# A graph-network kernel with a new order of its steps: both halves of the scores side by side, layer-one sums directly ahead of their product, other first and last steps

## The chip, the core and the metric

The kernel runs on one core of a Trainium2 chip. The core has four compute engines with a queue of their own each: TensorE (PE, matrix products into PSUM; its weight loads are listed as PEld), VectorE (DVE), ScalarE (ACT) and GpSimd (POOL). SyncE (SP) issues the DMA transfers. Engines meet through semaphores, and each works through its queue in order. The metric is the device time of the core in microseconds (us), lower is better; the shown time is the median of three runs.

## What is computed

64 graphs of 256 nodes with 512 features go through two layers, the second of which is two graph attentions in a row. In short:

```
# layer 0: 8 heads of 64
Q, K, V = x @ W_q, x @ W_k, x @ W_v
scores = einsum('bihd,bjhd->bhij', Q, K) / 8 + bias(x @ w_g) + log(adj + 1e-9)
x = einsum('bhij,bjhd->bihd', softmax(scores), V) + x
# layer 1, twice: 8 heads with W1, then 1 head with W2
h = layer_norm(x) @ W
e = leaky_relu(s_i + t_j, 0.2) + adj        # s, t: h times two vectors, per head
x = einsum('bhij,bhjk->bhik', softmax(e), h) + x
```

All is float32.

## The kernel before

Each graph (a "batch") is one Python generator, `graph(b)`; a call of `next` on it emits one *step*. The steps of a batch have names: load, turn (transposes X and the adjacency), V, V7, V4, Q, Q7, Q4, K, K7, K4, two scores, two mask, sums 0, product 0, gather 0, tokens 1, V1, V1 7, V1 4, rows 1, eight weights, sums 1, product 1, gather 1, tokens 2, V2, V2 7, V2 4, rows 2, weights 2, two product 2. The digit 0 stands for layer 0, 1 for the first attention of layer 1, 2 for the second.

What each step does, with the lines of the profile:

- V, Q, K, V1 and V2 are 256x512 by 512x512 products done in seven half-size products (Strassen and Winograd, `winograd`, matmuls on L326 or L333). The main step makes products 1, 5, 2, 6 and 3; product 6 adds into the bank ps_a that product 1 wrote, and product 3 into ps_b, so each must wait for ScalarE's copy of that bank (m and u: L525, L558 or L639). The step ending in 7 makes product 7, again into ps_a, after the copy u of product 6; the one ending in 4 makes product 4 into ps_a, after VectorE has read product 7 (L537, L567, L575 or L648). ScalarE reads product 4 (L535, L646 and others).
- A scores step (L592) makes four heads: 64-row matmuls, two at a time in the two halves of the array, into four PSUM banks. ScalarE takes exp of each bank (L599).
- A mask step multiplies the exps of four heads with the adjacency (L613, 128x1024, two of them) and adds the two halves up (L618).
- sums (L384) makes the sums of the weights over the source nodes with 32-column matmuls, four at a time; VectorE inverts them (L390), and the result goes to DRAM (L393) and comes back spread over partitions as R (L398). It also fetches the stored x (L252), to which ScalarE adds a bias (L409).
- product (L425) is weights times values, also 32-column matmuls. gather scales it with R (L434), adds x (L438), transposes (L258), takes statistics (eight L263, L265), and GpSimd makes the sums and differences S for the next Winograd product (L302 to L305). In layer 1, GpSimd also adds a row to the transposed Z (L702), after L265.
- tokens finishes the statistics: one matmul (L268), some ten small VectorE operations (L273 to L290), and a power on GpSimd (L292) that gives rstd.
- V1 4 ends with L659, which rows 1 needs: L458, L460, four stores (L463) and two loads (L473) of R, 512 KB each. A buffer for R is one of three, and is free again when sums 1 of the batch before has read it.
- weights: relu (L676), plus adjacency (L682), exp (L686), and at the end of four heads the sum of the two halves, written over R (L691).
- weights 2 is two operations on VectorE (L744); product 2 (L756) ends with a reciprocal (L761), a scaled copy (L764), an addition on GpSimd (L765) and four stores of the output (L771).

The batches overlap like a pipeline. A list `period` holds (age, step) pairs: in period n, step s with age a is emitted for batch n - a. It is repeated for all batches, but the first periods are replaced by a list `start`, and the last by `finish`, where the batch is counted from the end. TensorE works in exactly the order of these lists (`manual_schedule`); for the other engines the framework's planner orders the instructions from priorities and its own estimate of durations, so their orders change when the list does. All PSUM tiles come from one ring of eight banks.

```
period = [
    (1, "V4"), (2, "mask"), (5, "V2"), (5, "V2 7"), (2, "sums 0"),
    (2, "product 0"), (5, "V2 4"), (1, "Q"), (5, "rows 2"), (4, "sums 1"),
...
```

Of the kernel before, what the change touches and what calls it, by code (L numbers as in the profile page):

```python
# [20 lines left out]
def kernel(  # L21
# [94 lines left out]
    def weight(name, more=0):  # L116
        return const.tile([P, 2, 7, HD + more], F32, name=name)
# [34 lines left out]
    with ExitStack() as main:  # L152
# [324 lines left out]
        def graph(b):  # L477
# [295 lines left out]


        period = [
            (1, "V4"), (2, "mask"), (5, "V2"), (5, "V2 7"), (2, "sums 0"),
            (2, "product 0"), (5, "V2 4"), (1, "Q"), (5, "rows 2"), (4, "sums 1"),
            (3, "weights"), (2, "gather 0"), (3, "weights"), (3, "weights"),
            (5, "weights 2"), (3, "weights"), (0, "turn"), (1, "Q7"), (4, "product 1"),
            (1, "Q4"), (1, "K"), (1, "K7"), (5, "product 2"), (1, "K4"), (3, "weights"),  # L780
            (5, "product 2"), (2, "tokens 1"), (0, "V"), (1, "scores"), (3, "weights"),
            (3, "weights"), (2, "V1"), (4, "gather 1"), (-1, "load"), (2, "V1 7"),
            (0, "V7"), (4, "tokens 2"), (2, "V1 4"), (1, "scores"), (1, "mask"),
            (2, "rows 1"), (2, "weights"),
        ]

        start = [
            (0, "load"), (0, "turn"), (0, "V"), (0, "V7"), (0, "V4"), (1, "load"),
            (0, "Q"), (1, "turn"), (0, "Q7"), (0, "Q4"), (2, "load"), (0, "K"),
            (0, "K7"), (0, "K4"), (0, "scores"), (1, "V"), (1, "V7"), (1, "V4"),  # L790
            (2, "turn"), ("w1", "transpose"), (0, "scores"), (0, "mask"), (0, "mask"),
            (1, "Q"), (0, "sums 0"), (1, "Q7"), (0, "product 0"), (0, "gather 0"),
            (1, "Q4"), (1, "K"), ("w1", "columns"), (3, "load"), (1, "K7"), (1, "K4"),
            (3, "turn"), (0, "tokens 1"), ("w1", "totals"), (1, "scores"), (2, "V"),
            (2, "V7"), (0, "V1"), ("w2", "transpose"), (1, "scores"), ("w2", "columns"),
            (0, "V1 7"), (0, "V1 4"), (1, "mask"), (1, "mask"), (1, "sums 0"),
            (2, "V4"), (2, "Q"), (0, "rows 1"), (2, "Q7"), (2, "Q4"), (1, "product 0"),
            (2, "K"), (0, "weights"), (1, "gather 0"), (2, "K7"), (0, "weights"),
            (1, "tokens 1"), (2, "K4"), (2, "scores"), (3, "V"), (2, "scores"),
            (1, "V1"), (2, "mask"), ("w2", "totals"), (2, "mask"), (1, "V1 7"),  # L800
            (0, "weights"), (4, "load"), (2, "sums 0"), (0, "weights"), (0, "weights"),
            (1, "V1 4"), (0, "weights"), (0, "weights"), (3, "V7"), (1, "rows 1"),
            (2, "product 0"), (1, "weights"), (3, "V4"), (0, "weights"), (3, "Q"),
            (5, "load"), (3, "Q7"), (4, "turn"), (2, "gather 0"), (0, "sums 1"),
            (3, "Q4"), (3, "K"), (3, "K7"), (1, "weights"), (0, "product 1"), (3, "K4"),
            (2, "tokens 1"), (4, "V"), (2, "V1"), (1, "weights"), (0, "gather 1"),
            (1, "weights"), (1, "weights"), (2, "V1 7"), (1, "weights"), (3, "scores"),
            (1, "weights"), (2, "V1 4"), (1, "weights"), (4, "V7"), (0, "tokens 2"),
            (3, "scores"), (3, "mask"), (2, "rows 1"), (2, "weights"),
        ]  # L810
        FOLDS = [(w, step) for w in ("w1", "w2") for step in ("transpose", "columns", "totals")]
        order = [
# [3 lines left out]
        ]  # L816

        finish = [
            (-3, "mask"), (-6, "V2"), (-2, "V4"), (-6, "V2 7"), (-3, "sums 0"),
            (-3, "product 0"), (-6, "V2 4"), (-2, "Q"), (-5, "sums 1"), (-4, "weights"),  # L820
            (-4, "weights"), (-2, "Q7"), (-6, "rows 2"), (-5, "product 1"),
            (-4, "weights"), (-1, "turn"), (-3, "gather 0"), (-2, "Q4"), (-2, "K"),
            (-6, "weights 2"), (-2, "K7"), (-4, "weights"), (-6, "product 2"),
            (-2, "K4"), (-3, "tokens 1"), (-4, "weights"), (-6, "product 2"), (-1, "V"),
            (-2, "scores"), (-3, "V1"), (-3, "V1 7"), (-1, "V7"), (-5, "gather 1"),
            (-5, "tokens 2"), (-3, "V1 4"), (-4, "weights"), (-2, "scores"),
            (-3, "rows 1"), (-1, "V4"), (-2, "mask"), (-5, "V2"), (-4, "weights"),
            (-2, "mask"), (-5, "V2 7"), (-2, "sums 0"), (-4, "sums 1"),
            (-2, "product 0"), (-5, "V2 4"), (-3, "weights"), (-2, "gather 0"),
            (-1, "Q"), (-5, "rows 2"), (-4, "product 1"), (-1, "Q7"), (-1, "Q4"),  # L830
            (-1, "K"), (-3, "weights"), (-2, "tokens 1"), (-5, "weights 2"),
            (-5, "product 2"), (-1, "K7"), (-5, "product 2"), (-2, "V1"), (-1, "K4"),
            (-3, "weights"), (-3, "weights"), (-2, "V1 7"), (-3, "weights"),
            (-1, "scores"), (-3, "weights"), (-3, "weights"), (-2, "V1 4"),
            (-2, "rows 1"), (-4, "gather 1"), (-4, "tokens 2"), (-1, "scores"),
            (-1, "mask"), (-2, "weights"), (-4, "V2"), (-1, "mask"), (-3, "weights"),
            (-4, "V2 7"), (-1, "sums 0"), (-1, "product 0"), (-4, "V2 4"),
            (-4, "rows 2"), (-2, "weights"), (-2, "weights"), (-3, "sums 1"),
            (-1, "gather 0"), (-4, "weights 2"), (-3, "product 1"), (-2, "weights"),
            (-4, "product 2"), (-1, "tokens 1"), (-3, "gather 1"), (-4, "product 2"),  # L840
            (-1, "V1"), (-1, "V1 7"), (-2, "weights"), (-1, "V1 4"), (-1, "rows 1"),
            (-3, "tokens 2"), (-2, "weights"), (-2, "weights"), (-3, "V2"),
            (-1, "weights"), (-3, "V2 7"), (-3, "V2 4"), (-3, "rows 2"),
            (-1, "weights"), (-2, "weights"), (-2, "sums 1"), (-1, "weights"),
            (-3, "weights 2"), (-2, "product 1"), (-1, "weights"), (-1, "weights"),
            (-3, "product 2"), (-3, "product 2"), (-1, "weights"), (-2, "gather 1"),
            (-1, "weights"), (-2, "tokens 2"), (-1, "weights"), (-1, "sums 1"),
            (-1, "product 1"), (-2, "V2"), (-2, "V2 7"), (-2, "V2 4"), (-2, "rows 2"),
            (-2, "weights 2"), (-2, "product 2"), (-1, "gather 1"), (-1, "tokens 2"),
            (-2, "product 2"), (-1, "V2"), (-1, "V2 7"), (-1, "V2 4"), (-1, "rows 2"),  # L850
            (-1, "weights 2"), (-1, "product 2"), (-1, "product 2"),
        ]
        whole = start + order[len(start) - len(FOLDS) : len(order) - len(finish)]
        whole += [(B + g, name) for g, name in finish]
# [3 lines left out]
        with tc.manual_schedule(engines={mybir.EngineType.PE}):  # L858
# [3 lines left out]
            w1, w2 = weight("w1", H), weight("w2", 1)  # L862
# [52 lines left out]
    with ExitStack() as rest:  # L915
# [6 lines left out]
        def tl(name, *shape):  # L922
            return pool.tile(list(shape), F32, name=name, tag=name)
# [108 lines left out]
        with tc.For_i(0, again) as b:  # L1032
# [40 lines left out]
            V = tl("Vr", P, NT, D)  # L1073
# [50 lines left out]
```

## Time and profile before

| what | value |
|---|---|
| median of 3 runs | 3265.06 us (3260.84 to 3265.26) |
| profiled execution, its own time | 3264.86 us |
| its span | 3263.1 us |
| mean granted TensorE clock | 0.991 |
| DMA, mean over the span | 125 GB/s |

The costliest groups of the page read: line, engine, operation, tile written and tiles read, shape, count, then busy time and mean duration in ns, and at last the time in which the engine stood still just before, with what ended most of it. Four of them:

| line, engine | count | mean ns | still before it |
|---|---|---|---|
| L613 DVE | 256 | 1670 | 77.4 us, for ACT L599 |
| L676 ACT | 1024 | 501 | 85.0 us, mostly for PE L425 |
| L599 ACT | 512 | 684 | 96.6 us, for PE L592 |
| L691 DVE | 128 | 1261 | 8.2 us, for ACT L686 |

The timeline lists, per engine, start and duration in us, the line, the tiles and how many records were merged. TensorE's records overlap, so the time that an item takes from the next is the difference of two starts. A matmul in float32 shows as two records. From 200 us to 3100 us the pattern repeats about every 49 us, one period.

### The profile page before, as it was taken

The numbers are of one execution on the slowest core, as the hardware profiler recorded it, in microseconds if no ns is written. First come the engines' busy times: TensorE is split into PE (matmuls) and PEld (weight loads), VectorE is DVE, ScalarE is ACT, GpSimd is POOL, SyncE is SP. The second block draws the span as 40 slices with busy tenths as digits, with TensorE's granted clock in tenths as the row PEclk, the third lists the DMA queues.
The fourth block names the chain that finished last, engine by engine and source line by source line (L and its number), as shares of the span: only waits on it lengthen the run. The fifth ranks groups of instructions, "written<-read, shape, count | busy, mean of one in ns | idle before, by whom it ended". The sixth has DMA issues, their size and how long they took to land.

```text
span 3263.1 us, 77828 instructions
## 1 busy us (share of the span) xinstructions
PE 3172.2 (97%) x28232; PEld 2604.9 (80%) x28232; DVE 2700.9 (83%) x6093; ACT 2192.0 (67%) x5959; POOL 1077.0 (33%) x1315
## 2 busy tenths in 40 slices
PE   7999999999999999999999999999999999999985
PEld 5788888888888888888888888888888888888863
DVE  4888888888888888888888888888888888888884
ACT  2567667667667667667677677677677676676673
POOL 2233333332332342332332332332332332332332
PEclk9999999999999999999999999999999999999997
DMA  4334434444443444444443344444344344334332
GB/s 130 100 120 129 133 120 131 130 123 129 126 129 123 130 128 124 132 129 123 132 126 126 126 131 128 126 129 129 124 127 132 123 127 134 124 121 136 121 111 79
DMA packets 354662, 407.92 MB, mean 125 GB/s; under 512 B 117840, under 2 KB 262496, under 8 KB 354272
## 3 DMA queue, kind: packets, MB, share of 16 engines
q1 hardware_dynamic: 353120, 401.83, 39.7%
q8 instruction: 224, 3.67, 0.5%
q14 instruction: 166, 1.36, 0.1%
q10 hardware_dynamic: 1152, 1.06, 0.1%
HBM read 266.83 MB, written 135.87 MB: 123 GB/s over the span
## 4 chain that ended last, share of the span: by engine, by line
PE 86%; ACT 4%; DMA 3%; DVE 2%; issue 1%; SPq 0%; POOL 0%; DVEq 0%; ACTq 0%; POOLq 0%
PE ps_a L326 21%; PE ps_a L333 13%; PE ps_num L425 11%; PE ps_b L326 10%; PE ps_sc L592 7%; PE ps_av L756 7%; PE ps_b L333 6%; PE ps_c L326 5%; PE ps_su L384 4%; PE ps_c L333 3%; DMA R<-kept 2%; ACT ET L676 2%; ACT ET L686 1%; PE ps_st L268 1%; DMA zT<-kept 0%
## 5 line engine op out<-in xcount | busy, mean ns | idle before, releaser
L682 DVE TENSOR_TENSOR ET<-ET,AT 128x512 f32<-128x512 f32 x512 | 345.2, 685 | 234.7 <-ACT ET L676 234.5
L676 ACT ACTIVATE ET<-R,f 128x256 f32<-128x256 f32 x1024 | 460.5, 501 | 85.0 <-PE ps_num L425 70.1
L613 DVE TENSOR_TENSOR ET<-ET,AT 128x1024 f32<-128x1024 f32 x256 | 422.8, 1670 | 77.4 <-ACT ET L599 77.4
L686 ACT ACTIVATE ET<-ET,ends 128x256 f32<-128x256 f32 x1024 | 468.2, 503 | 11.7 <-DVE ET L682 4.9
L425 PE MATMUL ps_num<-ET,V 128*32 128x256 f32 x8192 | 467.5, 380 | 0.0
L302 POOL TENSOR_TENSOR S<-yT 128x256 f32<-128x256 f32 x64 | 47.4, 740 | 1112.0 <-DVE yT L438 994.6
L765 POOL TENSOR_TENSOR X<-X,weighted 128x256 f32<-128x256 f32 x256 | 211.7, 836 | 598.9 <-ACT weighted L764 598.8
L425 PEld LDWEIGHTS ps_num<-ET,V 128*32 128x32 f32 x8192 | 258.5, 110 | 162.1 <-issue 0.8
L599 ACT ACTIVATE ET<-ps_sc,V 128x512 f32<-128x512 f32 x512 | 309.0, 684 | 96.6 <-PE ps_sc L592 96.6
L756 PE MATMUL ps_av<-V,ET 128*128 128x258 f32 (+1 forms) x1024 | 252.7, 392 | 22.8 <-DVE ET L744 22.8
L326 PE MATMUL ps_a<-w,S 128*128 128x264 f32 (+1 forms) x1024 | 267.9, 384 | 3.9 <-ACT m L639 3.7
L326 PE MATMUL ps_b<-w,S 128*128 128x264 f32 (+1 forms) x1024 | 266.5, 383 | 0.0
L592 PE MATMUL ps_sc<-QT,KT 64*128 64x256 f32 x2048 | 258.3, 391 | 0.0
L592 PEld LDWEIGHTS ps_sc<-QT,KT 64*128 64x128 f32 x2048 | 188.5, 187 | 60.1 <-issue 41.7
L756 PEld LDWEIGHTS ps_av<-V,ET 128*128 128x128 f32 x1024 | 191.2, 197 | 47.5 <-issue 17.2
L263 DVE BATCH_NORM_STATS2 parts<-Z 128x6 f32<-128x128 f32 x1024 | 227.0, 275 | 0.0
L326 PEld LDWEIGHTS ps_a<-w,S 128*128 128x128 f32 x1024 | 188.9, 190 | 42.0 <-ACT m L639 5.4
L326 PEld LDWEIGHTS ps_b<-w,S 128*128 128x128 f32 x1024 | 193.9, 189 | 31.1
L646 ACT ACTIVATE V<-ps_a,rstd 128x257 f32<-128x257 f32 (+1 forms) x128 | 60.0, 469 | 205.0 <-PE ps_a L326 205.0
L409 ACT ACTIVATE yT<-yT,columns 128x256 f32<-128x256 f32 x256 | 115.0, 498 | 115.9 <-DMA yT<-kept 115.8
L434 DVE TENSOR_TENSOR ps_num<-ps_num,R 128x512 f32<-128x512 f32 x256 | 170.9, 692 | 5.5 <-DMA R<-kept 3.4
L691 DVE TENSOR_TENSOR R<-ET 128x1024 f32<-128x1024 f32 x128 | 161.4, 1261 | 8.2 <-ACT ET L686 8.1
(175 smaller groups left out, 7281.5 us busy)
## 6 DMA issues: line engine op xcount, KB each, us to landing
R<-kept SPq DMA_DIRECT2D x128, 512.0 KB
X<-in_x_dram SPq DMA_DIRECT2D x256, 128.0 KB
kept<-xT SPq DMA_DIRECT2D x64, 512.0 KB
yT<-kept SPq DMA_DIRECT2D x64, 512.0 KB
R<-kept SPq DMA_DIRECT2D x512, 64.0 KB
kept<-yT SPq DMA_DIRECT2D x64, 512.0 KB
kept<-Z SPq DMA_DIRECT2D x64, 512.0 KB
X<-kept SPq DMA_DIRECT2D x512, 64.0 KB
```

Source lines behind the costliest of these rows:

```text
L263: nc.vector.bn_stats(parts[:, block].rearrange("p h c -> p (h c)"), Z[:, block, :])
L326: nc.tensor.matmul(to, A[:, kk, :], B[:, kk, :], start=(first and kk == 0), stop=(kk == 1), skip_group_check=not first,)
L333: nc.tensor.matmul(to[:, m * P : (m + 1) * P], B[:, kk, m * P : (m + 1) * P], A[:, kk, :], start=(first and m == kk == 0), stop=(kk == 1), ...
L425: nc.tensor.matmul(num[32 * a : 32 * a + 32, m * N : (m + 1) * N], V[:, j, a // 2, a % 2 * P + q * DH + 32 * m :][:, :32], pair[a // 2][:, ...
L592: nc.tensor.matmul(banks[h % 2][:, o : o + N], KT[lo : lo + DH, (q + h) // 2, j * P : (j + 1) * P], QT[lo : lo + DH, (q + h) // 2, :], sta ...
L599: nc.scalar.activation(ET[:, j, i::2, :], banks[i].rearrange("p (h n) -> p h n", n=N), AF.Exp, bias=c[:, j, :],)
L613: nc.vector.tensor_tensor(ET[:, j, :, :], ET[:, j, :, :], AT[:, j, :].unsqueeze(1).to_broadcast([P, 4, N]), ALU.mult,)
L676: nc.scalar.activation(ET[:, j, h, :], R[q][:, h, :], AF.Relu, bias=f[:, j, at : at + 1])
L682: nc.vector.tensor_tensor(two, two, AT[:, j, :].unsqueeze(1).to_broadcast([P, 2, N]), ALU.add)
L686: nc.scalar.activation(ET[:, j, i, :], ET[:, j, i, :], AF.Exp, bias=targets[:, j, 4 * q + i : 4 * q + i + 1],)
L756: nc.tensor.matmul(av[:, :width], ET[:, j, t * P : (t + 1) * P], V2[:, j, n, :width], start=(j == 0), stop=(j == NT - 1),)
L765: nc.gpsimd.tensor_tensor(o[:, cols], o[:, cols], weighted, ALU.add)
```

## The change

Only the three lists differ; no operation is added or removed. In `period`:

- the two scores steps of a batch follow one another directly (they stood before and after V1 with its step 7), and stand ahead of V4;
- sums 1 stands directly ahead of product 1 on TensorE (the steps between them issue nothing there); before, Q7 was between them;
- Q7 follows Q, since sums 1 no longer comes there;
- V1 follows V (before, a scores step was between them), and V1 4 comes before tokens 2 (before, after it);
- both mask steps come behind both scores;
- weights, turn and load take other places.

```diff
         period = [
-            (1, "V4"), (2, "mask"), (5, "V2"), (5, "V2 7"), (2, "sums 0"),
-            (2, "product 0"), (5, "V2 4"), (1, "Q"), (5, "rows 2"), (4, "sums 1"),
-            (3, "weights"), (2, "gather 0"), (3, "weights"), (3, "weights"),
-            (5, "weights 2"), (3, "weights"), (0, "turn"), (1, "Q7"), (4, "product 1"),
-            (1, "Q4"), (1, "K"), (1, "K7"), (5, "product 2"), (1, "K4"), (3, "weights"),
-            (5, "product 2"), (2, "tokens 1"), (0, "V"), (1, "scores"), (3, "weights"),
-            (3, "weights"), (2, "V1"), (4, "gather 1"), (-1, "load"), (2, "V1 7"),
-            (0, "V7"), (4, "tokens 2"), (2, "V1 4"), (1, "scores"), (1, "mask"),
-            (2, "rows 1"), (2, "weights"),
+            (3, "V1 4"), (5, "tokens 2"), (2, "scores"), (2, "scores"), (1, "V4"),
+            (3, "rows 1"), (2, "mask"), (5, "V2"), (3, "weights"), (2, "mask"),
+            (5, "V2 7"), (2, "sums 0"), (2, "product 0"), (5, "V2 4"), (1, "Q"),
+            (5, "rows 2"), (1, "Q7"), (4, "sums 1"), (2, "gather 0"), (3, "weights"),
+            (3, "weights"), (3, "weights"), (5, "weights 2"), (4, "product 1"),
+            (0, "turn"), (1, "Q4"), (1, "K"), (1, "K7"), (3, "weights"),
+            (5, "product 2"), (1, "K4"), (5, "product 2"), (3, "weights"),
+            (2, "tokens 1"), (0, "V"), (2, "V1"), (3, "weights"), (4, "gather 1"),
+            (2, "V1 7"), (0, "V7"), (-1, "load"), (3, "weights"),
         ]
```

The lists `start` and `finish` are rewritten in the same sense. In `start`, the first scores of batch 1 come ahead of tokens 1 of batch 0, and rows 1 of batch 0 comes sooner:

```diff
-            (3, "turn"), (0, "tokens 1"), ("w1", "totals"), (1, "scores"), (2, "V"),
-            (2, "V7"), (0, "V1"), ("w2", "transpose"), (1, "scores"), ("w2", "columns"),
...
+            ("w1", "columns"), (0, "gather 0"), (2, "turn"), (1, "K4"), (1, "scores"),
+            (0, "tokens 1"), (3, "load"), (2, "V"), ("w1", "totals"), (4, "load"),
+            (0, "V1"), (2, "V7"), (0, "V1 7"), (0, "V1 4"), (2, "V4"),
+            ("w2", "transpose"), (1, "scores"), ("w2", "columns"), (0, "rows 1"),
...
```

In `finish`, V2 of the batch before the last stands ahead of sums 1 of the last, and product 1 of the last behind V2 4:

```diff
-            (-1, "weights"), (-2, "tokens 2"), (-1, "weights"), (-1, "sums 1"),
-            (-1, "product 1"), (-2, "V2"), (-2, "V2 7"), (-2, "V2 4"), (-2, "rows 2"),
-            (-2, "weights 2"), (-2, "product 2"), (-1, "gather 1"), (-1, "tokens 2"),
...
+            (-2, "tokens 2"), (-3, "product 2"), (-2, "V2"), (-1, "weights"),
+            (-1, "weights"), (-1, "weights"), (-1, "sums 1"), (-2, "V2 7"),
+            (-2, "V2 4"), (-2, "rows 2"), (-2, "weights 2"), (-1, "product 1"),
+            (-1, "gather 1"), (-2, "product 2"), (-1, "tokens 2"), (-2, "product 2"),
...
```

## The prediction

> **What bounds the kernel now.** I read the busy table first, then the chain of waits, then TensorE's timeline over a period, then the same stretch on VectorE and GpSimd.
>
> ```profile
> PE 3172.2 (97%) x28232; PEld 2604.9 (80%) x28232; DVE 2700.9 (83%) x6093; ACT 2192.0 (67%) x5959; POOL 1077.0 (33%) x1315
> PE 86%; ACT 4%; DMA 3%; DVE 2%; issue 1%; SPq 0%; POOL 0%; DVEq 0%; ACTq 0%; POOLq 0%
> ```
>
> TensorE (PE) is busy 97% and is 86% of the chain that ended last. Gaps can't be the prize, so I look for time that is lost while PE counts as busy. The timeline of PE (start, duration, line, tiles, records) shows it when starts are subtracted:
>
> ```profile
> 1505.83 1.03 PE L326 MATMUL ps_b<-wv,S 128*128 128x257 f32 x4
> 1506.79 2.00 PE L592 MATMUL ps_sc<-QT,KT 64*128 64x256 f32 x16
> 1508.72 1.16 PE L326 MATMUL ps_a<-w,yT 128*128 128x264 f32 x4
> 1509.71 1.05 PE L326 MATMUL ps_b<-w,S 128*128 128x264 f32 x4
> ...
> 1524.43 1.08 PE L384 MATMUL ps_su<-total,ones 128*32 128x128 f32 x32
> 1525.33 3.64 PE L425 MATMUL ps_num<-ET,V 128*32 128x256 f32 x64
> 1528.89 1.13 PE L326 MATMUL ps_a<-w,zT 128*128 128x257 f32 x4
> ...
> 1533.44 1.06 PE L333 MATMUL ps_b<-S,wq 128*128 128x128 f32 x8
> 1534.42 1.08 PE L384 MATMUL ps_su<-R,ones 128*32 128x128 f32 x32
> 1535.43 1.16 PE L333 MATMUL ps_a<-S,wq 128*128 128x128 f32 x8
> 1536.52 3.66 PE L425 MATMUL ps_num<-ET,V 128*32 128x256 f32 x64
> 1540.11 1.16 PE L333 MATMUL ps_a<-xT,wq 128*128 128x128 f32 x8
> 1541.11 1.06 PE L333 MATMUL ps_a<-xT,wk 128*128 128x128 f32 x8
> ...
> 1544.55 1.16 PE L333 MATMUL ps_a<-S,wk 128*128 128x128 f32 x8 [0.59 <-ACT m L525]
> ```
>
> A product of 128x257 takes 0.87 from start to start in a run of its kind (1504.10, 1504.96, 1505.83), one of 128x264 0.89, one of wq or wk 0.89. Ahead of the scores (64 rows) it takes 0.96, behind them 0.99. Going into the 64-row or 32-column layout and back (an "excursion") costs about 0.1 each way, and some inside.
>
> **The saving.** *Scores.* Cut into three stretches, a scores step is 0.32 for its first pair of records, 1.30 for six pairs (0.216 each), 0.31 for the last. Two apart: 0.09 in + 1.93 + 0.10 out, twice = 4.24. Side by side: 0.09 + (0.32 + 14 x 0.216 + 0.31 = 3.65) + 0.10 = 3.84. Saved: 0.40 a batch. *Layer-one sums and product.* Before, 1533.44 to 1541.11 holds product 3 of Q, sums, product 7, L425 and product 4: 7.67. After: 0.89 + 0.98 (product 7, going in) + 0.90 (sums straight into L425, as at 1524.43) + 3.58 + 1.00 = 7.35. Saved: 0.32. In the built order, the tiled stretches fall from 321 to 199: 60 pairs of scores merge and 62 of the others. 60 x 0.40 + 62 x 0.32 = 43.8, say **44 us**. The Trainium skill (TensorEngine Tiling (Array Packing), Performance Considerations) speaks against it: tiling speeds up TensorE, not the emptying of PSUM, which can then be the bottleneck. By that rule the two steps would last as long as ScalarE's eight exps: four at L599 take 2.42, eight some 4.75, against 3.65, so 1.1 x 60 = 66 us would be lost and the change be 22 slower. The row: at 0.58 an exp from 1.17 after the first matmul (1506.79, 1507.96) a bank is free at 1.85, and only the eighth bank (V's ps_a is held, seven are free) needs one, for the last quarter at 2.7. V4 behind them needs none, V2's three come after 4.6. So PE runs ahead and I take no stall; ScalarE's lag turns up below.
>
> **What the new order exposes.** Positions in us from V's first product, from the slots above: before, scores 4.4, V1 6.3, V1 4 12.9, scores 13.9, V2 16.7, layer-one sums 32.0, K 38.7. After: V1 4.4, V7 9.7, V1 4 10.6, statistics (L268) 11.5, both scores 11.8, V4 15.5, V2 16.4, layer-zero sums 21.7, Q 27.2, layer-one sums 32.6, K 38.1. A missed start costs the lateness and 0.1 for restarting (K's products after the 0.59 wait take 0.99).
>
> *(1) V1 directly behind V.* The scores no longer stand between, 1.93 of cover. Product 6 of V1, at 7.08, adds into ps_a and needs its copy (L639, 0.48). ScalarE's new order has the last two L686 ahead of that copy, and they need the last L682, which VectorE now has behind all eight L263 of zT. VectorE's small operations there meet GpSimd:
>
> ```profile
> 2049.71 3.15 DVE L613 TENSOR_TENSOR ET<-ET,AT 128x1024 f32<-128x1024 f32 x1 [0.16 <-ACT ET L599]
> 2049.41 2.36 POOL L702 TENSOR_TENSOR Z<-Z,bw 128x1024 f32<-128x1024 f32 x1 [0.60 <-DVE parts L263]
> 2059.62 1.23 DVE L613 TENSOR_TENSOR ET<-ET,AT 128x1024 f32<-128x1024 f32 x1 [1.01 <-ACT ET L599]
> ```
>
> The same L613 takes 3.15 beside L702 and 1.23 without. The Trainium skill (SBUF — State Buffer, section "SBUF: two separate sides") calls that port pair an exclusive lock, kept for a whole instruction. The rows' sum, unblocked: L258 1.16, two L768 0.1, eight L263 1.6, the statistics 0.6 and L537 0.34 from -0.45 put L682 (0.6) at 3.4 to 4.0, the copy done at 6.0 behind V1's own first product: no wait. By the lock, L768, L284, L285 and L288 each wait out what is left of one of GpSimd's 0.72 operations (L303 to L765, 0.0 to 4.2), some 1.8 together: L682 ends near 5.85, two L686 at 6.85, the copy at 7.3. I take **0.3** (0.2 late, 0.1 restart); ends 0 and 0.9 (every one a full turn late).
>
> *(2) L691 and the three L648.* L691 comes behind L265, which releases L702, so it takes some 3 instead of 1.26; L648 for V1 4 ends at 10.7 against 10.6. With (1) PE is itself 0.3 late: 0; ends 0 and 0.3.
>
> *(3) Layer-zero sums.* All mask work now stands behind the pair: from 2.46 after the scores' start four L613 and two L618 at 1.14 a turn, without L702, bound by exps 2 and 8, end at 9.5; the sums come at 9.9. If GpSimd's S for zT holds VectorE's small chain as now (2.6 against 1.4), 9.9: **0.05**; ends 0 and 0.3. Gone is the 2.36-long block of L613 by L702, worth nothing, since PE did not wait for it.
>
> *(4) Q7 directly behind Q.* Before, the sums (1.01) lay between and covered u (L558, two of 0.31). Product 6 ends 0.16 after its slot, u 0.62 and its signal later: 0.85 of 0.89, too late for loading weights ahead. **0.15**; ends 0 and 0.25.
>
> *(5) Layer-one R.* The layer-one sums release the buffer that SP's second L473 waits for; queued behind it are L473 of layer two, L393, yT's store and four L398, whose R VectorE's L434 takes 8.6 later. Sums end at 33.5 instead of 33.05, K is 0.6 earlier: 1.1 less room. But between R's landing and K's first copy ScalarE now has four L676 and two L686 instead of five and four, 1.2 less. K's present stall (a mean period of 49.17, from the layer-zero sums at 197.07 and 3097.92 over 59 periods, against 48.80 from 2016.15 to 2064.95) stays: 0; ends -0.2 and 0.2. The other moved issues (load, and the out-stores, 1 and 7 around xT's store instead of 2 and 6) stand in front of transfers for which PE never waits in the waits view: 0.
>
> *(6) First and last steps.* In the first 200 us PE waits about 31, in the last 110 about 40. Scores of batch 1 now cover part of the 3.9 wait at 84.17, while V1 of batch 0 comes nearer to its folded weights: 0. At the end V2 of batch -2 runs ahead of the last product instead of after (3209 instead of 3215), but the last sums come as much later: -4; ends -12 and +8.
>
> Sum: 3264.86 (profiled run; span 3263.1) - 44 + 60 x 0.50 - 4 = **3247 us**, -0.55%. The profiled run lies 0.2 under the shown median 3265.06, so no shift.
>
> **The rivals.** *A, cover holds:* VectorE and ScalarE keep ahead, only Q7's 0.15 stays: 3264.9 - 44 + 9 - 4 = 3226. For it: VectorE has slack (83%) and L691 leaves the stretch ahead of V. Against: the lock's row. *B, slower:* the chain L682, L686, copy, product 6. If L682 starts behind L702 or every small operation waits out a GpSimd turn, (1) is 0.9, the sums 0.3 and Q7 0.15, with 0.05 more at V1 4: 1.4 x 60 = 84, so 3265 - 44 + 84 - 4 = 3301. It decides from 0.8 a batch on. For it: five of 0.72 in a row; against: the operations now waiting mostly slip into the next gap. *C, nothing shown:* the waits move along with PE to R's landing, 0.75 a batch in all: 3264.9 - 44 + 45 - 4 = 3262. For it: the 0.59 wait in K; against: room computed in (5).
>
> **How the numbers follow.** Forecast 0.43 (3232 to 3258), A 0.17, B 0.27, C 0.13. Measurements of this kernel tell 0.2% (6.5 us) from no change. Faster: 0.43 + 0.17 = 0.60; same 0.13; slower 0.27. The range leaves out the lower part of A and B's upper half: 3214 to 3292.
>
> **What would show it.** Right: two scores steps together last 3.65, L384 goes into L425 after 0.90 both times, and product 6 of V1 starts 0.2 to 0.4 late behind ACT m L639. A: that start is on time, the period 48.1 to 48.2. B: PE waits for ACT m L639 or DVE total L618 over 0.6 a period. Wrong altogether, if sums and L425 side by side keep 1.01 and 3.59.

## The result, and the profile after

The changed kernel takes **3236.28 us** (median of 4 runs, 3234.22 to 3239.5), the kernel before in the same comparison 3265.16 (4 runs, 3260.84 to 3266.13): a ratio of 0.9915, 95% interval [0.9898, 0.9932]. The forecast was 3247: the right side, 11 us too slow. The profiled execution's span went from 3263.1 to 3232.4 at the same granted clock, 0.991.

The busy table and the chain of the page after, which answer to the two lines shown first in the prediction, and two of its groups (busy, mean ns, idle time before and its releaser):

```profile
PE 3135.6 (97%) x28232; PEld 2621.6 (81%) x28232; DVE 2717.1 (84%) x6093; ACT 2188.5 (68%) x5959; POOL 1068.4 (33%) x1315
...
PE 1%; DVE 1%; DMA 0%; ACT 0%; SPq 0%; issue 0%; POOL 0%; DVEq 0%
...
L686 ACT ACTIVATE ET<-ET,ends 128x256 f32<-128x256 f32 x1024 | 482.1, 503 | 104.7 <-DVE ET L682 103.6
...
L613 DVE TENSOR_TENSOR ET<-ET,AT 128x1024 f32<-128x1024 f32 x256 | 306.6, 1231 | 39.4 <-ACT ET L599 39.4
```

TensorE is busy 36.6 us less (3172.2 before) with the same 28232 matmuls, and still 97% of the span: what went was time inside "busy". The chain is of no use this time: it could be followed back over some 2% of the span only. Two groups changed: ScalarE's L686 now waits 103.6 us for VectorE's L682 (4.9 before), and L613 fell from 1670 to 1231 ns a piece.

TensorE's timeline of the kernel after, in one period (start, duration, line, tiles, records):

```profile
2016.95 1.14 PE L333 MATMUL ps_a<-S,wq 128*128 128x128 f32 x8
2018.03 1.08 PE L384 MATMUL ps_su<-R,ones 128*32 128x128 f32 x32
2018.93 3.64 PE L425 MATMUL ps_num<-ET,V 128*32 128x256 f32 x64
2022.49 1.16 PE L333 MATMUL ps_a<-xT,wq 128*128 128x128 f32 x8
2023.49 1.06 PE L333 MATMUL ps_a<-xT,wk 128*128 128x128 f32 x8
2024.38 1.06 PE L333 MATMUL ps_b<-S,wk 128*128 128x128 f32 x8
2025.28 1.06 PE L333 MATMUL ps_c<-xT,wk 128*128 128x128 f32 x8
2027.18 1.16 PE L333 MATMUL ps_a<-S,wk 128*128 128x128 f32 x8 [0.85 <-ACT m L525]
...
2040.82 1.05 PE L326 MATMUL ps_c<-w,yT 128*128 128x264 f32 x4
2041.71 1.05 PE L326 MATMUL ps_a<-w,S 128*128 128x264 f32 x4
...
2046.14 0.32 PE L268 MATMUL ps_st<-parts,same 128*128 128x48 f32 x2
2046.39 3.72 PE L592 MATMUL ps_sc<-QT,KT 64*128 64x256 f32 x32
```

Subtract starts. Q7 starts on time, 0.89 after the product ahead of it; from Q7 to the sums is 1.08, the sums go into L425 after 0.90, and L425 takes 3.56 to the next product: the three figures of the merge. Product 6 of V1 (2041.71) comes 0.89 after product 2: it does not wait. Product 6 of K (2027.18) comes 1.90 after product 2, where 0.89 is its clean slot.

The same subtraction, as the mean of the 51 periods between 400 and 2900 us, with what the prediction's slots and latenesses come to:

| slot (start to next start), us | before | after | forecast |
|---|---|---|---|
| two scores steps, without entry and exit | 2 x 1.93 | 3.654 | 3.65 |
| Q7 to layer-one sums | - | 1.074 | 1.13 |
| layer-one sums, layer-zero sums, each to the next item | 1.01 (Q7), 0.90 | 0.897, 0.897 | 0.90 |
| product 2 to 6 of V1 (copy L639) | 0.89 | 0.890 | 1.19 |
| V1 4 and L268, up to the scores | 1.21 | 1.14 | - |
| K, products 2 to L756 (four slots) | 4.07 | 4.27 | 4.07 |

The mean period, from the third product of one V to that of the next over 55 periods, fell from 49.165 to 48.702, by 0.463; over some 58 periods that is 26.9 of the 30.7 by which the span fell. The rest comes from the two ends: the third product of the sixth V lies at 232.8 instead of 225.5 (7.3 lost), and from that of the last V to the end it takes 174.7 instead of 185.9 (11.2 gained).

Where did the new stall in K come from? ScalarE's timeline of the kernel after, around the same product 6 of K (in brackets: idle time before, and its releaser):

```profile
2022.14 0.91 ACT L686 ACTIVATE ET<-ET,ends 128x256 f32<-128x256 f32 x2 [0.33 <-DVE ET L682]
2023.86 1.71 ACT L676 ACTIVATE ET<-R,f 128x256 f32<-128x256 f32 x4 [0.81 <-DMA R<-kept]
2025.47 0.90 ACT L686 ACTIVATE ET<-ET,ends 128x256 f32<-128x256 f32 x2
2026.27 0.60 ACT L558 ACTIVATE QT<-ps_a,columns 128x128 f32<-128x128 f32 x2
2026.77 0.36 ACT L525 COPY m<-ps_a 128x256 f32<-128x256 f32 x1
2027.02 0.38 ACT L525 COPY m<-ps_b 128x256 f32<-128x256 f32 x1
2027.29 0.52 ACT L686 ACTIVATE ET<-ET,ends 128x256 f32<-128x256 f32 x1
2027.70 0.72 ACT L517 ACTIVATE AT<-AT,eps 128x512 f32<-128x512 f32 x1
2028.31 0.51 ACT L686 ACTIVATE ET<-ET,ends 128x256 f32<-128x256 f32 x1
2028.71 0.37 ACT L525 COPY u<-ps_a 128x256 f32<-128x256 f32 x1
```

K's first product ended near 2024.5, but its copy m ran at 2026.77, behind four L676 of the second half (which waited for R's landing at 2023.86), two L686 of the first half and two copies of QT. Before, in the period that the prediction shows (K's first product started at 1541.11), ScalarE's row was this:

```profile
1540.03 2.11 ACT L676 ACTIVATE ET<-R,f 128x256 f32<-128x256 f32 x5 [0.84 <-DMA R<-kept]
1542.04 1.69 ACT L686 ACTIVATE ET<-ET,ends 128x256 f32<-128x256 f32 x4
1543.63 0.60 ACT L558 ACTIVATE QT<-ps_a,columns 128x128 f32<-128x128 f32 x2
1544.13 0.36 ACT L525 COPY m<-ps_a 128x256 f32<-128x256 f32 x1
```

From the first L676 behind R to copy m the row is shorter now, 2.91 instead of 4.10, as (5) forecast. But that L676 starts 0.37 after K's first product instead of 1.08 ahead of it. R's landing can be dated in every period by the semaphore that this L676 waits for: on average it came 1.67 ahead of K's first product before, and comes 0.28 ahead now, 1.39 later. In the kernel after, the slot with the wait for m follows the landing closely (correlation 0.97 over 52 periods). In 38 of these periods the row starts within 0.05 of the landing; in the other 14 R is there, and the row starts directly behind the two L686 that stand ahead of it.

The waits of ScalarE, in total, times and longest, for the kernel after; before they were 4.9 (6 times) and 13.6 (20 times):

```profile
ACT ET L686 <- DVE ET L682: 103.6, 120, 2.1
ACT ET L676 <- DMA R<-kept: 18.9, 26, 3.4
```

The first total misleads when it is read as K's. By place in the period, 79 of the 103.6 us (59 waits) lie 15 to 17 us behind K's first product, ahead of V1's copies, where TensorE does not wait (slot 0.890). Ahead of K there are 17.5 us, 52 waits of 0.34, all before the row that starts with R's L676.

So there were four theories of K's stall to part. **T1**: the landing of R. **T2**: VectorE's L682 come late and hold L686, which hold the copies. **T3**: only the place of m in ScalarE's queue. **T4**, formed on the way: ScalarE's whole row of work from R's landing to u.

### The profile page after: what moved, and what is told of

Its sections match the earlier page's. It is cut to its first block, busy times and chain, and to the rows that moved or that the text cites. A ratio compares the mean times of both kernels' runs of the same rounds, so it can differ in the third digit from the quotient of the medians.

```text
span 3232.4 us, 77827 instructions
## 1 busy us (share of the span) xinstructions
PE 3135.6 (97%) x28232; PEld 2621.6 (81%) x28232; DVE 2717.1 (84%) x6093; ACT 2188.5 (68%) x5959; POOL 1068.4 (33%) x1315
## 5 line engine op out<-in xcount | busy, mean ns | idle before, releaser
L682 DVE TENSOR_TENSOR ET<-ET,AT 128x512 f32<-128x512 f32 x512 | 363.4, 711 | 239.3 <-ACT ET L676 238.7
L686 ACT ACTIVATE ET<-ET,ends 128x256 f32<-128x256 f32 x1024 | 482.1, 503 | 104.7 <-DVE ET L682 103.6
L676 ACT ACTIVATE ET<-R,f 128x256 f32<-128x256 f32 x1024 | 461.3, 501 | 74.9 <-PE ps_num L425 55.7
L425 PE MATMUL ps_num<-ET,V 128*32 128x256 f32 x8192 | 466.7, 379 | 0.0
L765 POOL TENSOR_TENSOR X<-X,weighted 128x256 f32<-128x256 f32 x256 | 210.9, 834 | 545.0 <-ACT weighted L764 536.9
L425 PEld LDWEIGHTS ps_num<-ET,V 128*32 128x32 f32 x8192 | 263.9, 110 | 155.2 <-issue 1.1
L613 DVE TENSOR_TENSOR ET<-ET,AT 128x1024 f32<-128x1024 f32 x256 | 306.6, 1231 | 39.4 <-ACT ET L599 39.4
L599 ACT ACTIVATE ET<-ps_sc,V 128x512 f32<-128x512 f32 x512 | 302.3, 697 | 7.8 <-PE ps_sc L592 7.8
L756 PE MATMUL ps_av<-V,ET 128*128 128x258 f32 (+1 forms) x1024 | 250.7, 389 | 24.3 <-DVE ET L744 24.3
L592 PE MATMUL ps_sc<-QT,KT 64*128 64x256 f32 x2048 | 239.4, 383 | 0.0
L263 DVE BATCH_NORM_STATS2 parts<-Z 128x6 f32<-128x128 f32 x1024 | 238.3, 275 | 0.1
L756 PEld LDWEIGHTS ps_av<-V,ET 128*128 128x128 f32 x1024 | 189.8, 196 | 48.9 <-issue 13.0
L326 PEld LDWEIGHTS ps_a<-w,S 128*128 128x128 f32 x1024 | 185.9, 189 | 46.7 <-ACT m L639 6.9
L702 POOL TENSOR_TENSOR Z<-Z,bw 128x1024 f32<-128x1024 f32 x64 | 175.7, 2745 | 4.1 <-DVE parts L263 3.0
```

Of the source, the lines that this page charges most:

```text
L263: nc.vector.bn_stats(parts[:, block].rearrange("p h c -> p (h c)"), Z[:, block, :])
L326: nc.tensor.matmul(to, A[:, kk, :], B[:, kk, :], start=(first and kk == 0), stop=(kk == 1), skip_group_check=not first,)
L425: nc.tensor.matmul(num[32 * a : 32 * a + 32, m * N : (m + 1) * N], V[:, j, a // 2, a % 2 * P + q * DH + 32 * m :][:, :32], pair[a // 2][:, ...
L592: nc.tensor.matmul(banks[h % 2][:, o : o + N], KT[lo : lo + DH, (q + h) // 2, j * P : (j + 1) * P], QT[lo : lo + DH, (q + h) // 2, :], sta ...
L599: nc.scalar.activation(ET[:, j, i::2, :], banks[i].rearrange("p (h n) -> p h n", n=N), AF.Exp, bias=c[:, j, :],)
L613: nc.vector.tensor_tensor(ET[:, j, :, :], ET[:, j, :, :], AT[:, j, :].unsqueeze(1).to_broadcast([P, 4, N]), ALU.mult,)
```

## The experiments

All times are medians of several runs; each ratio is to the kernel before on the same chip, with its 95% interval. The kernel before read 3262 to 3268 in these comparisons, so compare ratios. Lines of a kernel with added code are shifted by a few.

### Is the saving the layout?

**One scores pair taken apart again**, with V4 between; everything else as after.

```diff
-            (2, "scores"), (2, "scores"), (1, "V4"),
+            (2, "scores"), (1, "V4"), (2, "scores"),
```

> The changed kernel with one step moved: V4 stands between the two scores steps instead of behind them, so that TensorE leaves the 64-row layout and returns once more in each period. Theory (going into and out of a tiled layout costs 0.40 us for the scores): 60 periods x 0.40 = 24 us more than the changed kernel, some 3260 us, and two scores steps of 1.93 in place of one of 3.65. Rival (the change gains by other waits, and the layout is not what is paid): within 5 us of the changed kernel's 3236.

Measured: 3262.71, ratio 1.0001 [0.9991, 1.0010]; mean period 49.130, 0.43 more than after, and K's slots and ScalarE's waits nearly as after. By its own slots the pair is worth 0.40 a period (the rest is mostly K's slots, 4.33 here): 23 to 25 of the 29 us.

**Layer-one sums apart from their product again**, with Q7 between, as before.

```diff
-            (5, "rows 2"), (1, "Q7"), (4, "sums 1"), (2, "gather 0"), (3, "weights"),
+            (5, "rows 2"), (4, "sums 1"), (1, "Q7"), (2, "gather 0"), (3, "weights"),
```

> The changed kernel with the layer-one sums back between Q and Q7; Q7 then stands between sums and product again. Theory of the layout: +0.32 a period, less 0.09 for the late start of Q7 that goes, so +0.23 x 62 = 14 us if the stall in K stays; the sums come 1.0 us sooner, so if K's stall comes from the R that waits for them, K's first copy is up to 1.0 sooner and the stall (0.43 a period in the changed kernel) goes: then -12 us or so against the changed kernel's stall, a sum of about 3238. If the stall in K comes from VectorE alone, 3250.

Measured: 3251.07, ratio 0.9962 [0.9948, 0.9976]; mean period 48.934, 0.23 more than after. That is the merge of 0.32 less the 0.09 by which Q7 takes longer directly behind Q. K's four slots together stayed (4.29), though R now landed 1.65 ahead of K's first product (0.28 in the kernel after): the first wait shrank (its slot 1.33 to 1.01), as T1 has it, and the wait of product 7 for u took its place (0.96 to 1.34), ScalarE's row behind R being longer in this order. So an earlier R alone does not shorten K.

### What holds K?

**The second R fetched as two transfers of two heads each**, so that the first heads land sooner.

```diff
-                nc.sync.dma_start(out=R, in_=kept[q : q + n, :].partition_broadcast(P))
+                for i in range(0, n, 2 if q else n):
+                    m = min(2, n) if q else n
+                    nc.sync.dma_start(
+                        out=R[:, i : i + m], in_=kept[q + i : q + i + m, :].partition_broadcast(P)
+                    )
```

> The changed kernel, with the second R of a batch loaded in two transfers of two heads each instead of one of four, so that its first half lands about 2 us sooner after the layer-one sums. Theory T1 (the stall in K of the changed kernel is the landing of R): ScalarE's waits for R (18.9 us) nearly go, and the stall in K falls from 0.43 to 0.1 a period: -15 to -20 us, about 3219. Theory T2 (it is VectorE's late L682, behind L258 and under GpSimd's lock): the stall stays within 0.1, the time within 5 us of 3236; one more issue on SP costs nothing that shows.

Measured: 3262.9, ratio 0.9998 [0.9988, 1.0008]. ScalarE waits longer for R, not shorter: 44.3 us in 59 waits (18.9 in 26). The planner, told that R's first heads come sooner, put their L676 sooner, and they waited. K's four slots went from 4.27 to 4.74; 0.47 x 60 = 28 accounts for the whole loss against the kernel after. The run missed both expectations and settles nothing between T1 and T2, but shows that ScalarE's built order decides.

**gather 0 listed behind three weights steps**, to let VectorE's L682 run ahead of it. TensorE's order is that of after.

```diff
-            (4, "sums 1"), (2, "gather 0"), (3, "weights"),
-            (3, "weights"), (3, "weights"), (5, "weights 2"),
+            (4, "sums 1"), (3, "weights"), (3, "weights"),
+            (3, "weights"), (2, "gather 0"), (5, "weights 2"),
```

> The changed kernel with gather 0 listed two weights steps later. TensorE's order is the same; the planner gives VectorE's L682 of these weights a place ahead of L258 and the eight L263, and ScalarE its four L686 before the second R. T2 (ScalarE waits for VectorE's L682: 103.6 us in the changed kernel, 4.9 in the one before): these waits in K fall below half, K's stall from 0.43 to about 0.2 a period, some 3222. T1 (R's landing): waits for R stay or grow, the stall in K stays above 0.35, 3236.

Measured: 3271.16, ratio 1.0029 [1.0018, 1.0040]. TensorE's wait in K in this kernel:

```profile
PE ps_a L333 <- ACT u L525: 60.8, 59, 1.1
```

The wait for m is gone (slot 0.90), R is waited for 4.9 us only, and now product 7 waits for u in every period (slot 2.11): in the built order four L676, an L686 and L517 stand between K's first copy and u. Four slots of K: 4.91. R lands as late as in the kernel after (0.24 ahead of K's first product, 0.28 there), but ScalarE now comes to the L676 that need it later than that, so that they rarely wait. The stall is larger without any wait for R: T1 cannot be the whole of it. This is where T3 came from.

**Sums directly behind Q, Q7 behind product 1.**

```diff
-            (5, "rows 2"), (1, "Q7"), (4, "sums 1"), (2, "gather 0"), (3, "weights"),
+            (5, "rows 2"), (4, "sums 1"), (2, "gather 0"), (3, "weights"),
...
-            (0, "turn"), (1, "Q4"), (1, "K"), (1, "K7"), (3, "weights"),
+            (0, "turn"), (1, "Q7"), (1, "K"), (1, "Q4"), (1, "K7"), (3, "weights"),
```

> The order after, with sums 1 directly behind Q (as in the Q7 trial), so R's buffer is free sooner, Q7 between turn and K (its copy u covered by product 1), and Q4 between K and K7. PE's layout changes are as in the order after. T3 (what makes K late is the place of K's copies in ScalarE's queue, behind second-half L676 that wait for R): in the built order K's copy m now stands behind eight L676 of the second half instead of four, so K waits more, and with it product 7 behind u: period 48.9 to 49.2, time 3248 to 3266. Rival T1 (R's landing alone): sums a product earlier give R 0.9 more room, the wait in K falls by 0.3 a period: 3218.

Measured: 3469.06, ratio 1.0637 [1.0619, 1.0655]. One premise was wrong: a batch emits its steps in its own order whatever their names in the list, so what ran was Q7, Q4, K, K7. TensorE's timeline of this kernel:

```profile
2065.62 1.16 PE L333 MATMUL ps_a<-S,wq 128*128 128x128 f32 x8
2069.07 1.16 PE L333 MATMUL ps_a<-xT,wq 128*128 128x128 f32 x8 [2.29 <-DVE QT L567]
...
2086.13 1.05 PE L326 MATMUL ps_c<-w,yT 128*128 128x264 f32 x4
2088.21 1.16 PE L326 MATMUL ps_a<-w,S 128*128 128x264 f32 x4 [1.03 <-ACT m L639]
```

Two covers are gone. Product 4 of Q stands directly behind product 7 and waits for VectorE to read it (3.47 instead of 0.89); and product 6 of V1 waits for copy m L639 in every period (2.08 instead of 0.89). It is the product whose wait the prediction priced at 0.3 and made rival B of, but the way there is another: the copy waits for rstd (L292; 213.6 us in 63 waits), which waits for the statistics, and among these L285, an operation on two elements a partition, now runs beside GpSimd's L702:

```profile
2083.63 2.28 DVE L285 SCALAR_TENSOR_TENSOR var<-means,var 128x2 f32<-128x2 f32 x1
```

It took about 2.28 in 58 of its 128 executions and 0.12 to 0.15 in most others. The two lost covers make 3.8 of the 4.1 by which the mean period grew, to 52.79. K's own slots fell to 3.91, but this says little about T3.

**The second half's L676 kept behind K's copies.** An edge of issue order on ScalarE alone; no data is waited for less. In one run they come behind the second m, in the other behind u.

```diff
...
+                    behind = [m for m in copies if len(m) > 1] if at >= 4 else []
+                    with tc.issue_after(behind[-1][1]) if behind else nullcontext():
-                    for j in range(NT):
+                        for j in range(NT):
...
```

> The order after, and one edge of issue order on ScalarE: no L676 of the second half is issued ahead of K's second copy m (the one product 3 needs). It takes no wait for data away and does not touch R, its buffer or VectorE's work. T3 (place in the queue): the wait for R no longer stands ahead of m, K's stall (0.45 a period over the clean 0.89) goes but for what the copies of QT and the last two L686 of the first half leave: period 48.3 to 48.4, time 3213 to 3219. Rival T1 (R's landing): the same lateness is paid behind m instead, by copy u or by the L682 and L686 that V1's copies stand behind: 3230 to 3240. Rival T2 (L682 late on VectorE holds L686, and L686 the copies): two L686 still stand ahead of m: 3225 to 3236.

> As the run before, but no L676 of the second half is issued ahead of K's copy u either (the one product 7 needs); they come some 2.6 later. T3: K's products wait for nothing but L686 of the first half: period 48.25 to 48.35, 3210 to 3216, unless the second half's later L682 and L686 now hold the copies of V and V1 (they stand between them in the built order): then up to 0.4 a period is paid there, 3216 to 3236. T1: no gain, 3230 to 3240.

Measured: 3472.57, ratio 1.0648 [1.0630, 1.0665], and 3453.21, ratio 1.0579 [1.0561, 1.0596]. No theory had this. In K, T3 was right for the first wait: its slot fell from 1.33 to 0.94 and 0.95. In the first run the wait went over to u (product 3's slot 0.96 to 1.43, four slots 4.39); behind u as well, the four slots make 3.84. But the planner then laid VectorE's work out anew. TensorE's timeline at V1 of the second run, and VectorE's and GpSimd's beside it:

```profile
2074.38 1.03 PE L326 MATMUL ps_a<-wv,S 128*128 128x257 f32 x4
2077.71 1.16 PE L326 MATMUL ps_a<-w,yT 128*128 128x264 f32 x4 [2.30 <-DVE V L656]
```
```profile
2073.36 1.44 DVE L263 BATCH_NORM_STATS2 parts<-Z 128x6 f32<-128x128 f32 x7
2074.72 0.47 DVE L656 SCALAR_TENSOR_TENSOR V<-ps_b,rstd,u 128x264 f32<-128x264 f32 x1
2075.11 2.15 DVE L265 TENSOR_TENSOR parts<-parts 128x16 f32<-128x16 f32 x1
2077.18 0.48 DVE L656 SCALAR_TENSOR_TENSOR V<-ps_a,rstd,m 128x264 f32<-128x264 f32 x1
```
```profile
2074.88 2.34 POOL L712 TENSOR_TENSOR Z<-Z,bw 128x1024 f32<-128x1024 f32 x1 [3.84 <-DVE parts L263]
```

With the L682 later, zT's scaling, transpose and statistics come later too, and L265 now runs just ahead of the read of product 7 (L656, which is L648). L265 has 128x16 elements and takes 2.15, because GpSimd's L712 (L702) runs beside it. Product 4 waits 2.30 in nearly every period (138.0 us in 65 waits). 0.4 a period was won in K and some 4 lost here, at the next scores and at V1's product 6.

The loss at the scores is one of the clock. The two scores steps directly behind such a wait, in two periods of this run:

```profile
1974.23 5.40 PE L600 MATMUL ps_sc<-QT,KT 64*128 64x256 f32 x32
2078.95 3.72 PE L600 MATMUL ps_sc<-QT,KT 64*128 64x256 f32 x32
```

In the first period the granted clock is 0.5 from 1974.2 to 1977.6, in the second it is not lowered. In the three runs that lost 6% (the one before and these two) it falls to half 22, 19 and 22 times between 400 and 2900 us, mostly for 3.4 us; 57 of these 63 times follow within 2.5 us on a wait of TensorE of over 2 us, which these runs have in every period. In the kernel after, the longest wait in that time is 1.7, and the clock is not lowered once. The mean scores slot rises with it from 3.65 to 4.26 and 4.35, and in the run before these two, K's first two products take 1.21 and 1.22 instead of 0.89.

**K's copies given a higher priority for the planner.** Only ScalarE's order changes: m stands ahead of the two copies of QT.

```diff
+            def copy_k(d, s, row, column):
+                with tc.high_priority(offset=100):
+                    nc.scalar.copy(d, s)
...
-            for _ in winograd(left, wk, False, copy, put_k):
+            for _ in winograd(left, wk, False, copy_k, put_k):
```

> The order after, with K's copies (m, m, u) given a higher priority for the planner. In the built order this moves one thing: on ScalarE, K's first m stands ahead of the two copies of QT (0.31 each) instead of behind them; VectorE's, GpSimd's, SyncE's and TensorE's orders are those of after. T3 (K waits for the place of its copies in ScalarE's queue): m comes 0.62 sooner; taken from each period's slot in the trace of after (0.98 to 2.78, mean 1.33, not under 0.89), the mean slot falls by 0.35: period 48.35, time 3215 to 3219. If the wait in K only moves to the products behind it (to the second m, for product 3, or to u, for product 7), the time stays at 3230 to 3236.

Measured: 3240.12, ratio 0.9910 [0.9896, 0.9924], after's own ratio. TensorE's timeline of this kernel, again in K:

```profile
2031.02 1.16 PE L333 MATMUL ps_a<-S,wk 128*128 128x128 f32 x8 [0.65 <-ACT m L579]
2032.02 1.06 PE L333 MATMUL ps_b<-S,wk 128*128 128x128 f32 x8
2033.47 1.16 PE L333 MATMUL ps_a<-S,wk 128*128 128x128 f32 x8 [0.40 <-ACT u L579]
```

The first slot fell by 0.22 on average, that of product 3 grew by 0.41: the wait went over to u, four slots 4.41. T3 in the form "m's place" is wrong, and T4 took its place: m and u are held by one row of ScalarE's work that starts with R's landing.

**That row shortened by L517**, which goes to GpSimd; two L676 that the planner would put in its place are kept behind u. The first steps are those of the kernel before.

```diff
-                nc.scalar.activation(AT, AT, AF.Identity, bias=eps)
+                nc.gpsimd.tensor_scalar(AT, AT, eps, None, ALU.add)
...
+                    behind = [m for m in copies if len(m) > 2] if at >= 6 else []
+                    with tc.issue_after(behind[-1][2]) if behind else nullcontext():
```

> As the last run with K's copies ahead of QT's and the first steps of the kernel before, and two edits more, after which VectorE's and SyncE's orders are still the same: the addition of 1e-9 to the adjacency (L517, 0.72 on ScalarE, between m and u of K) goes to GpSimd, and two L676 that the planner then puts in its place are kept behind u. ScalarE has two L686 left between m and u. T4 (what holds K is ScalarE's row of work from the landing of R to u as a whole, so that moving m alone only hands the wait to u): u comes 0.6 sooner, product 7's slot falls from 1.33 (after K's m was moved) towards 0.9 to 1.0, the period to 48.3 to 48.4: 3208 to 3216. Rivals: the two L686 wait for VectorE's L682 and hold u as before, or the GpSimd operation holds VectorE's port: no gain or a loss, 3225 to 3245.

Measured: 3232.81, ratio 0.9893 [0.9876, 0.9909]. The wait for u is gone, as T4 said (slot 1.34 to 0.89; four slots of K 3.76 against 4.27 in the run with the same first steps and L517 left in place, which comes last below), while R lands as late as there (0.32 and 0.30 ahead of K's first product). And yet the period is only 0.07 shorter, 48.63, which is within the scatter given below; T4's 48.3 to 48.4 did not come. Slot by slot, 0.15 of the gain is given back between L268 and V, 0.13 around L756 in product 2, and 0.16 in V and V1. Whether these are latenesses that K's stall had covered, or the price of giving GpSimd L517, is not shown: one wait that grew, of V's copy u for GpSimd's addition at L765 (67.7 us in 50 waits, 5.4 in 4 in that run), speaks for the second. ScalarE's waits for VectorE's L682 ahead of K are alike in both runs, 18 us, so that K's gain does not come from them (against T2).

### The first and last steps

**The first steps of before with the period and last steps of after**, and **the last steps of before with the rest of after** (the steps between are those of the period, less those that a list already holds).

```diff
         start = [
-            (0, "load"), (0, "turn"), (0, "V"), (0, "V7"), (0, "V4"), (0, "Q"),
+            (0, "load"), (0, "turn"), (0, "V"), (0, "V7"), (0, "V4"), (1, "load"),
...
```

> The order after with the list of first steps of the kernel before; period and last steps as after. By the trace of after, the first five periods cost 7 more than before (fifth V at 232.8 instead of 225.5): 3229 to 3231. If the steps that the period's own order asks for make up the difference, so that the old list runs into the new period no better: 3236. The forecast's figure for the start (0) would give 3236 too.

> The order after with the list of last steps of the kernel before; period and first steps as after. By the traces, from the last V's third product to the end it took 185.9 before and 174.6 after: the old last steps should cost 11: 3246 to 3248. By the forecast's figure (4): 3240. If the old steps lose nothing behind the new period: 3236.

**K's copies ahead of QT's, and the first steps of before:**

> K's copies ahead of QT's, as in the run beside it, and the list of first steps of the kernel before. If the two gains are independent (0.35 a period, and the 7.9 that the first steps gave alone): 3207 to 3212. If the first gain moves to other waits: 3222 to 3229.

Measured: old first steps 3228.36, ratio 0.9895 [0.9878, 0.9911]; old last steps 3249.06, ratio 0.9939 [0.9926, 0.9953]; both of the third 3234.22, ratio 0.9897 [0.9882, 0.9912]. In the traces the third product of the sixth V lies at 223.9 with the old first steps (232.8 after), and the end comes 184.9 after that of the last V with the old last steps (174.7 after, but 178.0 in the run with the old first steps, whose last steps are those of after). So the new first steps cost 7 to 9 and the new last ones win 7 to 11. By the times alone neither is settled (the intervals of 0.9895 and 0.9939 both overlap that of 0.9915). The mean period scatters by 0.1 between traces with the same period (48.70 in the kernel after, 48.74 and 48.81 in the first two runs here), some 6 us, which is in these times. The third run adds nothing to the first, as the run with K's copies alone suggested.

The best times come from the old first steps with the new period and the new last ones, with or without the edits around L517: 0.9895 and 0.9893 cannot be told apart, and the kernel after, 0.9915, is not clear of either.

## Why the prediction was right, and where it was not

*The saving, 44 us.* Right in its mechanism and size: 0.40 and 0.32 a period in the forecast; when each was undone, 0.40 by the slots (0.43 by the mean period) and 0.32 (0.23 with Q7's 0.09). A further 0.07 the forecast had missed: L268 stood ahead of V1 4, which then took 1.05 up to the scores, 1.21 together; now it stands between V1 4 and the scores, 0.89 and 0.25, 1.14 together.

*The Trainium skill's rule against it* (TensorEngine Tiling (Array Packing), Performance Considerations) did not decide here: the two scores steps take 3.654 in every period of the kernel after, while the eight exps take 4.72 (2047.83 to 2052.55 in the period shown). PE runs ahead of them, as the row of banks had it.

*(1) V1 directly behind V, 0.3 a period.* **Did not come**, 18 us of the miss. The lock acted as described: in the period shown L284 took 0.49 and L285 0.60, against 0.15 and 0.12 some 11 us later, with GpSimd idle; but L288, the last of the four, met no operation of GpSimd (0.14). So L682 ended 5.5 after V's first product instead of 5.85, the copy 6.8 instead of 7.3, and it was wanted at 7.08: 0.3 to spare, in a chain that had 0.2 too little by the forecast. That such waits can reach TensorE is real: with Q7 moved behind product 1, the same product waited 1.2 in every period, though by rstd and not by L682.

*(2)* 0, right in number: V1 4 waits for nothing (the last L648 ends 10.5 after V's first product, V1 4 starts at 10.6). Its reason was wrong: L702 is released by the last L263 (it starts 0.08 after it) and not by L265, as the prediction had it. In the period shown below L691 took 1.21, not 3, and it is L265 that waits out L702 (2.38). *(3)* 0.05 forecast, none seen (slot 0.960 in every period). *(4)* Q7 behind Q, 0.15 forecast, 0.09 measured: Q7 starts on time and takes 1.074 to the sums where 0.98 is clean.

*(5) K's stall stays: 0.* **This step failed**, in one term of its sum. K's four slots went from 4.07 to 4.27, 0.20 a period. Two terms came as forecast: from the end of the layer-one sums (the start of what follows them on TensorE) to K's first product 5.67 became 4.56 (1.11 less room, forecast 1.1), and from R's landing to K's copy m ScalarE takes 2.99 instead of 4.18 (1.19 less, forecast 1.2). The third the forecast took as unchanged: R landed 4.00 after the end of the sums before, and lands 4.29 after it now. 1.11 + 0.29 - 1.19 = 0.21, the 0.20 of the slots. Of the 0.29, 0.11 passes before SP issues the transfer and 0.18 from issue to landing; why is open. So the place and the sum of the stall are shown. No edit tried here took a single cause away with profit: each that took one wait out of K (R's, m's place) gave it to u or to another engine. Only keeping R's L676 behind u, or shortening ScalarE's row, took the stall out of K; the first lost 6% elsewhere, the second gained nothing clear of noise. A fourth buffer for R would part the landing from the sums; it was not tried.

*(6) The ends, -4.* The sum came out (7.3 lost, 11.2 won: -3.9), but by luck: the start was taken as 0 and the end as 4.

Put together by period: 0.40 + 0.32 + 0.07 saved, 0.09 + 0.20 lost, 0.50 in all against 0.463 by the mean period (0.485 over the 51 periods of the table). Two errors of opposite sign (0.3 too much at V1, 0.2 too little at K), with 0.05 too much for each of (3) and (4) and the 0.07 of L268, come to 0.27; the forecast's own gain of 0.23 a period falls 0.23 short of the measured one, 14 us over 60 periods, and the time was missed by 11. That the miss is so small is in part luck: K's 0.20 cancelled most of V1's 0.3.

## What to carry to other kernels

Where the busiest engine is 97% busy, subtract starts in its timeline and look for kinds of work that cost more at their borders than inside: putting two such stretches together paid what the slots said, 0.40 and 0.32 a period. A stall on an engine fed by three others can have several causes that are nearly equally late: take one away, and measure every slot of the period, not the one that you edited. In three runs here some 0.4 a period came back in other slots (0.38, 0.41 and 0.44). And split a total of waits by its place in the period before you take it for a cause: three quarters of the 103.6 us stood where they cost nothing. And where a planner orders the other engines, compare the built orders before a run is read: edits meant for one queue (a split transfer, a step listed elsewhere, an issue edge) came with changed orders of other queues, and lost time there.

## What the hardware showed unexpectedly

The exclusive lock between VectorE and GpSimd that the prediction read from L613 weighs most, by ratio, on small operations. VectorE's and GpSimd's timelines of the kernel after:

```profile
2039.44 0.67 DVE L682 TENSOR_TENSOR ET<-ET,AT 128x512 f32<-128x512 f32 x1
2040.04 2.38 DVE L265 TENSOR_TENSOR parts<-parts 128x16 f32<-128x16 f32 x1
2042.33 0.41 DVE L537 TENSOR_TENSOR V<-ps_b,u 128x257 f32<-128x257 f32 x1
```
```profile
2039.60 2.77 POOL L702 TENSOR_TENSOR Z<-Z,bw 128x1024 f32<-128x1024 f32 x1
```

L265 (16 elements a partition, 0.17 where GpSimd is idle) begins inside L702 and ends with it, at 2042.4: 2.2 of waiting, more than L613 lost before (3.15 less 1.23 = 1.9). Before, L265 stood directly behind the last L263, began just ahead of L702 and took 0.18; now an L682 stands between, and L702 is first. In the kernel after nothing is queued behind L265 that TensorE wants soon, and it costs nothing; where the read of product 7 stood behind it, product 4 waited 2.3 a period. L285, with two elements a partition, went from 0.12 to 2.28 in the same way in one run. L613, free of L702 now, fell by 0.44 on average and won nothing.
